# Two more turns in the hand-written matmul order, key norms read by strips, and a new order of small matmuls in each steady turn of a windowed-attention layer

## The chip, the cores and the metric

The kernel runs on one core of one Trainium2 chip, in fp32. The metric is the device time of one execution in microseconds (us), as the median of several runs. A core has TensorE (PE, matrix products), VectorE (DVE), ScalarE (ACT), GpSimd (POOL) and SyncE (SP, which here issues the DMAs). [...] the other data lies in SBUF, and large or rearranged data in DRAM.

## The reference, cut to what matters

The network has four layers and is run on two images ("batches"). The change touches only the first layer, an attention in which every pixel looks at the 3x3 pixels around it ("taps") and at pooled tokens of the whole image. Cut to what matters:

```python
q = (xf @ W_q + b_q).reshape(B, N, nh, hd).transpose(0, 2, 1, 3)
q_norm = _l2norm(q)
q_scaled = (q_norm + query_embedding[None]) * jax.nn.softplus(temperature)[None]
kv = xf @ W_kv + b_kv
...
k_l = _l2norm(k_l.reshape(B, N, nh, hd)).reshape(B, N, C)
...
attn_local = jnp.einsum('bhnd,bhndk->bhnk', q_scaled, k_local)   # k_local: 3x3 shifts of k
...
attn_pool = jnp.einsum('bhnd,bhpd->bhnp', q_scaled, _l2norm(k_pool))
attn = jax.nn.softmax(jnp.concatenate([attn_local, attn_pool], axis=-1), axis=-1)
a_local, a_pool = (attn[..., :ll], attn[..., ll:])
lt = jnp.einsum('bhnd,hdk->bhnk', q_norm, learnable_tokens) + learnable_bias[None] + a_local
x_local = jnp.einsum('bhnk,bhndk->bhnd', lt, v_local)             # v_local: 3x3 shifts of v
x_pool = jnp.einsum('bhnp,bhpd->bhnd', a_pool, v_pool)
xo = (x_local + x_pool).transpose(0, 2, 1, 3).reshape(B, N, C)
out = (xo @ W_proj + b_proj).reshape(B, C, H, W)
```

There are 512 channels, 8 heads of 64 channels, and 64x64 = 4096 pixels.

## The kernel before, in words

**Tiling.** A 128-channel group holds two heads. The pixels of one group are cut into four pieces of 1024 (`UT`), each of two blocks of 512 (`TB`). A piece of a group is a *unit*; there are 16, and each runs through a pipeline of stages. The loop in `run` (L2045 to L2090) makes turns i = -4 to 16. In turn i several stages work on different units: the projections make queries and keys of unit i+3 (and values of unit i+1), the tap products and tap sums belong to unit i+1, the attention to unit i, and the weighing of the taps to unit i-1.

**Stages**, with the lines that the text speaks of:
- `projections` (matmuls of `project`, L134: four per block of 512; ScalarE takes them out of PSUM, with squares for the norms, L2370 to L2376, values L2472). In a steady turn the order is first key block ("k0"), second key block ("k1"), the two query blocks, with values between.
- `norms` (L2410 to L2435): one matmul group sums the squares, which marks the start of a turn in what follows. VectorE makes inverse roots (L2413 to L2425). The inverses of the keys go by DMA to a small DRAM array, `inverse` (L2434); those of the queries are spread by a matmul and multiplied in by `normed` (L2445, L2448), and `learned` then multiplies the queries with the learned tokens (L2462, taken out at L2465) and scales them (L2467).
- `tap_products` and `tap_sums`: ScalarE copies the scaled queries to PSUM (L2483), VectorE multiplies them with shifted keys (L2489; in steady turns two taps in one instruction, the ninth alone, into two product buffers in turn). TensorE sums each product over the channels of a head (L2527) into the one "tap" bank, in pairs of taps. The bank is then multiplied by the inverse key norms, read back from DRAM (`tap_inverses`, L2513, L2536), and ScalarE takes its exponential (L2538).
- `attend`: scores with the pooled tokens (L2555), exponentials (L2559), values (L2565, copied out at L2567). GpSimd adds halves of the exponentials (L2574). The denominators are summed by matmuls (L2581 from the halves, L2584 from the taps). VectorE turns them (L2609), inverts (L2611), turns them back (L2612), multiplies the taps' weights (L2616) and adds the learned products (L2617). The weights are then spread by DMA to the rows of a heads' buffer (L2622).
- `weigh`: for each of ten rows of weights (the pooled part and nine taps), the row is fetched by DMA, spread over 64 partitions (`fetch_tap`, L2640). ScalarE copies its two halves into two PSUM banks (L2656), VectorE multiplies each with the shifted values (L2664; L2661 for the first row), and GpSimd adds the result to the unit's output (L2669). The finished unit is stored (L2675).
- `output` (L2252 to L2258): the layer's last product, from turn 14 on.

**What sets the order.** `in_turn` (L51) asks the stages of a turn in round robin for their next step, so each `yield` in a stage shifts what it issues after it by a step. In turns with `self.steady` set, TensorE's instructions keep exactly that order (`manual_schedule` on PE). The order on every other engine, and on TensorE in the other turns, is made by a scheduler from its own estimates. Tiles come from pools: five PSUM banks are shared by projections, scores, values, denominators, learned products and the copies of `weigh`; a matmul that takes a bank waits until its former user has been read. Each engine takes its instructions in order. SP issues its DMAs in order too.

**The inverse norms in DRAM.** `inverse` has, for each group of 128 channels, six rows of 4096 pixels with a margin: for two heads the three shifts by one column, all written by one DMA per block (row i is the same data, one element further). To scale the tap sums, twelve DMAs per unit read six rows each (four tile positions times three shifts by one image row).

Of the kernel before, what the change touches and what calls it, by code (L numbers as in the profile page):

```python
# [18 lines left out]
KC = C // P  # L19
# [1948 lines left out]
class Local:  # L1968
# [9 lines left out]
    def __init__(self, net, X, Y, sp_scale, d, wp, yp, pp, ppt, pps):  # L1978
        self.net, self.nc, self.vec, self.cst = net, net.nc, net.vec, net.cst
        self.X, self.Y, self.sp_scale, self.d = X, Y, sp_scale, d  # L1980
        self.wp, self.pp, self.ppt, self.pps = wp, pp, ppt, pps
        nc, new = self.nc, lambda shape, name: wp.tile(shape, F32, name=name)

        self.yd = yp.tile([P, KC, N], F32, name="yd")
        self.edge = W + 1
        self.inverse = yp.tile([6 * KC, N + 2 * self.edge], F32, name="inverse")
        self.wd = yp.tile([3, P, KC, C], F32, name="wd")
        self.rows = cycle([yp.tile([P // 2, self.UT], F32, name=f"rows{i}") for i in range(2)]).__next__

        R = W + 2  # L1990
        flat = Y.rearrange("p k n -> p (k n)")
        self.next_w = flat[:, :KC * C].rearrange("p (kc o) -> p kc o", kc=KC)
        whole = Lent(flat)
        self.kx, self.vx = (whole.take([P, R, R]) for _ in range(2))
        qs, self.kraw = whole.take([P, 3 * self.UT]), whole.take([P, self.UT])
        self.qs = [qs[:, i * self.UT:(i + 1) * self.UT] for i in range(3)]
        weighed = whole.take([P, 2 * self.UT])

        self.taps = ([weighed[:, i * self.UT:(i + 1) * self.UT] for i in range(2)]
                     + [new([P, self.UT], "tap2")])  # L2000
        self.prods = [new([P, 2, self.UT], f"prods{i}") for i in range(2)]
        self.tok = whole.take([P, KC, 32])
        late = new([P, 13 * TB + 3 * TB], "late")
        part = Lent(late)
        self.prob = part.ring([P, TB], 4)
        self.att = part.ring([P, self.UT], 2)
        self.els = part.ring([P, TB], 2)

        self.halves = [part.take([P, TB]) for _ in range(2)]
        self.recip = part.take([P, TB])  # L2010
        self.lts = part.ring([P, TB], 3)

        self.first = Lent(late[:, :12 * TB])
        self.gelus = Lent(late[:, 13 * TB:]).ring([P, TB], 3)
        self.raw_w = [w.rearrange("p (kc o) -> p kc o", kc=KC)
                      for w in (weighed, flat[:, 6144:8192])]
        self.w_sr = qs[:, :KC * C].rearrange("p (kc o) -> p kc o", kc=KC)
        self.fold = flat[:, :6144].rearrange("p (i kc o) -> p i kc o", i=3, kc=KC)
        self.kp = new([P, KC, NK], "kp")
        self.vp = new([P, 2, C], "vp")  # L2020
        self.qn = whole.take([P, self.UT])
        self.w3 = new([P, 3, KC, P], "w3")
        self.sq = [new([P, TB], f"sq{i}") for i in range(4)]
        self.half = new([P, 32], "mhalf32")
        self.qb = new([P, KC], "qe_scaled")
        self.bias = {i: new([P, KC], "b_" + i) for i in "qkv"}
        self.w, self.lt, self.el, self.out = {}, {}, {}, {}
        load = lambda w, src: nc.sync.dma_start(w, src.rearrange("(kc p) o -> p kc o", p=P))
        load(self.w_sr, d["W_sr"])
        for i, src in enumerate((d["W_q"], d["W_kv"][:, :C], d["W_kv"][:, C:])):  # L2030
            load(self.fold[:, i], src)
        for i in range(2):
            load(self.raw_w[i], d["W_kv"][:, i * C:(i + 1) * C])
        nc.sync.dma_start(self.tok, d["tok32"])
        nc.vector.memset(self.half, -0.5)

        nc.vector.tensor_tensor(self.qb, self.vec[:, V_QE:V_QE + KC], sp_scale, ALU.mult)
# [9 lines left out]
    def run(self):  # L2047


        self.nmean = self.net.stats[:, 0]  # L2050
        xs = self.pooled_tokens()
        heads = self.pooled_heads(xs)
        units = KC * self.UN
        unit = lambda u: u if 0 <= u < units else None
        self.pending = []
        for i in "qkv":
            self.fetch(i, 0)
        for i in range(-4, units + 1):
            made, ahead, u, before = (unit(i + n) for n in (3, 1, 0, -1))
            self.steady = 1 <= i < units - 4  # L2060
            streams, ended = [], []
            stages = [self.norms(streams, ended)]
            if ahead is not None:
                stages.append(self.tap_products(ahead))
            if u is not None:
                stages.append(self.attend(u))
            if i == units:
                stages.append(self.output(KC - 2))
            if before is not None:
                stages.append(self.weigh(before))  # L2070
            if ahead is not None:
                stages.append(self.tap_sums(ahead))
            values = ([ahead] if i > 0 and ahead is not None else
                      {-4: [0], -2: [1]}.get(i, []))
            stages.append(self.projections(made, values, streams))
            stages.append(self.normed(ended))
            if i < -2:
                stages.append(islice(heads, 12 if i == -4 else None))
            if i == units - 3:
                stages.append(self.fetch_output())  # L2080
            if units - 3 < i < units:
                stages.append(self.output(i - units + 2))
            if self.steady or i == units:
                with self.net.tc.manual_schedule(engines={mybir.EngineType.PE}):
                    in_turn(*stages)
            else:
                in_turn(*stages)

        self.nc.sync.dma_start(self.next_w, self.d["w_q1"].rearrange("(kc p) o -> p kc o", p=P))
        in_turn(self.output(KC - 1))  # L2090
# [3 lines left out]
    def pooled_tokens(self):  # L2094
# [35 lines left out]
                nc.sync.dma_start(self.wd[i], w3)  # L2130
        self.frame(self.kx)
        nc.gpsimd.memset(self.kraw[:, :TB], 0.0)
        for at in (0, self.edge - 1 + N):
            nc.sync.dma_start(self.inverse[:, at:at + self.edge + 1],
                              self.cst[:6 * KC, :self.edge + 1])
        return xs

    def pooled_heads(self, xs):
# [220 lines left out]
    def projections(self, u, uvs, streams):  # L2359
# [25 lines left out]

            uvs = [last - 1, last]
        values = [(u, j) for u in uvs for j in range(2)]
        made, taken = ((4, 6, 7, 8), (0, 2)) if self.steady else ((6, 7, 8, 9), (0, 3, 6, 9))
        for step in range(10):
            if step in made:  # L2390
                i = made.index(step)
# [8 lines left out]
    def norms(self, streams, ended):  # L2400
# [25 lines left out]
        for s, (which, u, j, part, _) in enumerate(before):  # L2426
            row = rows[32 * s:32 * s + 2, :]
            if which == "q":
                ended.append((s, row, u, j, part))
                continue  # L2430
            at = self.edge + 1 + u % self.UN * self.UT + j * TB
            a = self.inverse[u // self.UN * 6:][:2, at:at + TB]
            heads, cols = a.ap
            nc.sync.dma_start(bass.AP(a.tensor, a.offset, [heads, [2 * heads[0] - 1, 3], cols]),  # L2434
                              bcast(row, 1, 3))  # L2435
        yield

    def normed(self, ended):

        nc = self.nc  # L2440
        for _ in range(3 if self.steady else 5):
            yield
        mine = [(e, self.bank()) for e in ended]
        for (s, rows, *_), ps in mine:
            nc.tensor.matmul(ps, self.cst[32 * s:32 * s + 2, C_ROW:C_ROW + P], rows, start=True,  # L2445
                             stop=True)
        for (*_, part), ps in mine:
            self.multiplied = nc.vector.tensor_tensor(part, part, ps, ALU.mult).ins  # L2448
        for _ in range(3 if self.steady else 2):
            yield  # L2450
        if mine:
            self.learned(mine[-1][0][2])
        yield
# [52 lines left out]
    def tap_inverses(self, u):  # L2506
# [1 line left out]
        inverse = (self.kraw[:, :TB] if u < KC * self.UN - 1  # L2508
                   else self.w3[:, 2].rearrange("p k o -> p (k o)"))
        for q in range(4):  # L2510
            for dy in range(3):
                at = u % self.UN * self.UT + q // 2 * TB + dy * W + 1
                self.nc.sync.dma_start(inverse[32 * q + 6 * dy:][:6, :],  # L2513
                                       self.inverse[u // self.UN * 6:][:6, at:at + TB])
        return inverse

    def tap_sums(self, u):
# [24 lines left out]
    def attend(self, u):  # L2542
# [58 lines left out]
            halved(1)  # L2601
        yield
        values(1)
        yield
        if not self.steady:
            yield
        psD = sums()

# [7 lines left out]
        nc.vector.tensor_tensor(el, el, self.recip, ALU.mult)  # L2616
        nc.vector.tensor_tensor(el, el, self.lt.pop(u), ALU.add)  # L2617
        if self.steady:
            yield
        self.spread = self.rows()  # L2620
        for j in range(2):
# [244 lines left out]
```

## Time and profile before

| | us |
|---|---|
| median of 3 runs | 5019.44 (5018.5 to 5019.69) |
| the profiled execution | 5015.88 |
| its span in the trace | 5014.0 |
| a steady turn of layer 0 (turn 6, batch 0) | 41.48 |
| turn 11, turn 12 (start to next start) | 43.76, 51.05 |
| turn 13's start to the first output matmul (L2258) | 50.66 |
| TensorE busy in the span | 4771.4 |

In the trace layer 0 of the first batch has its steady turns (1 to 11) from 305.5 us to 764.1 us of the span, and the first output matmul at 865.8 us; the second batch's layer 0 lies later in the span and has the same turns. The page gives busy time by engine, 40 slices, DMA queues, a chain of waits, and groups of instructions. The other views are answers of the trace: busy time of every engine in given stretches, the instructions of one engine in order of time, and the waits of a stretch. In a timeline line stand the start, the duration, the engine, the line of the code, the operation and its tiles, the number of instructions joined in the line ("x2"), and in brackets the idle time before it and what ended that. In a line of waits stand the waiting engine and line, what released it, the sum in us, the number and the longest.

### The profile page before, as it was taken

The numbers are of one execution on the slowest core, as the hardware profiler recorded it, in microseconds if no ns is written. First come the engines' busy times: TensorE is split into PE (matmuls) and PEld (weight loads), VectorE is DVE, ScalarE is ACT, GpSimd is POOL, SyncE is SP. The second block draws the span as 40 slices with busy tenths as digits, with TensorE's granted clock in tenths as the row PEclk, the third lists the DMA queues.
The fourth block names the chain that finished last, engine by engine and source line by source line (L and its number), as shares of the span: only waits on it lengthen the run. The fifth ranks groups of instructions, "written<-read, shape, count | busy, mean of one in ns | idle before, by whom it ended". The sixth has DMA issues, their size and how long they took to land. (4 is left out here: it accounts for less than half of the span.)

```text
span 5014.0 us, 48290 instructions
## 1 busy us (share of the span) xinstructions
PE 4771.4 (95%) x16883; PEld 1971.8 (39%) x16883; DVE 3074.1 (61%) x3958; ACT 1816.8 (36%) x3477; POOL 1859.1 (37%) x1220
## 2 busy tenths in 40 slices
PE   7999998999999999999999999989999999999998
PEld 3433332554334444433343333335543344444333
DVE  4367776744679533477732777767446794335776
ACT  1256664244323233322112566642443242333221
POOL 0046665501320145554500466654014101554554
PEclk9999999999999999999999999999999999999999
DMA  3035555500000000211120455555000000000111
GB/s 154 1 103 155 155 156 164 160 19 10 1 17 0 1 1 1 72 55 44 58 74 2 126 154 157 151 159 150 12 10 1 17 1 1 1 1 24 43 45 43
DMA packets 129440, 313.29 MB, mean 62 GB/s; under 512 B 23394, under 2 KB 36194, under 8 KB 127652
## 3 DMA queue, kind: packets, MB, share of 16 engines
q1 hardware_dynamic: 129188, 310.12, 21.6%
q8 instruction: 135, 2.21, 0.2%
q14 instruction: 117, 0.96, 0.1%
HBM read 260.73 MB, written 49.31 MB: 62 GB/s over the span
## 5 line engine op out<-in xcount | busy, mean ns | idle before, releaser
L134 PE MATMUL mm<-big,w 128*128 128x512 f32 x2496 | 1164.9, 610 | 16.3 <-DVE big L2448 11.5
L134 PEld LDWEIGHTS mm<-big,w 128*128 128x128 f32 x2496 | 452.6, 191 | 698.3 <-issue 557.2
L2669 POOL TENSOR_TENSOR late<-late,big 128x1024 f32<-128x1024 f32 x194 | 458.5, 2363 | 223.4 <-DVE big L2664 185.4
L2489 DVE TENSOR_TENSOR prods<-qs,big 128x1024 f32<-128x1024 f32 (+1 forms) x200 | 332.2, 1686 | 60.1 <-PE tap L2527 49.1
L1669 POOL TENSOR_TENSOR big<-big 128x512 f32<-128x512 f32 x224 | 277.8, 1273 | 219.4 <-ACT big L1660 219.4
L2664 DVE TENSOR_TENSOR big<-big,mm 128x512 f32<-128x512 f32 x388 | 253.1, 681 | 114.9 <-ACT mm L2656 107.0
L1660 ACT ACTIVATE big<-mm,ed 128x256 f32<-128x256 f32 x512 | 193.5, 489 | 233.1 <-DVE top L1656 200.7
L2656 ACT COPY mm<-big 128x512 f32<-128x512 f32 x432 | 245.8, 597 | 60.4 <-DMA big<-rows 25.1
L2574 POOL TENSOR_TENSOR late<-late 128x512 f32<-128x512 f32 x84 | 105.3, 1275 | 410.5 <-ACT late L2559 393.9
L2669 POOL TENSOR_TENSOR late<-late,tap 128x1024 f32<-128x1024 f32 x94 | 222.1, 2363 | 94.5 <-DVE tap L2664 80.1
L1472 POOL TENSOR_TENSOR wq<-prob 128x512 f32<-128x512 f32 x48 | 71.6, 1515 | 487.9 <-ACT prob L1469 476.5
L1656 DVE TENSOR_REDUCE top<-mm 128x1 f32<-128x512 f32 x256 | 159.0, 684 | 148.1 <-PE mm L1587 148.1
L1924 PE MATMUL mm<-k,w 128*128 128x512 f32 x512 | 235.1, 602 | 12.4 <-DVE k L1917 7.5
L134 PE MATMUL mm<-big,wq 128*128 128x512 f32 x512 | 236.7, 608 | 2.7 <-ACT off_t L1243 2.7
L1215 PE MATMUL mm<-big,wo 128*128 128x512 f32 x512 | 238.1, 611 | 0.0
L1382 PE MATMUL acc<-big,diag 128*128 128x512 f32 x512 | 228.7, 604 | 9.8 <-ACT diag L1387 4.6
L1634 PE MATMUL mm<-w,big 128*128 128x512 f32 x512 | 234.5, 601 | 0.0
L973 POOL TENSOR_TENSOR group_stats<-group_stats,cst 128x1 f32<-128x1 f32 (+1 forms) x20 | 20.2, 1025 | 566.4 <-DVE group_stats L972 510.2
L2527 PE MATMUL tap<-prods,cst 128*32 128x512 f32 x1152 | 189.6, 620 | 29.2 <-ACT late L2538 26.5
L1914 DVE RECIPROCAL psD<-psD 128x512 f32<-128x512 f32 x64 | 215.1, 3362 | 1.9
L134 PE MATMUL mm<-big,big 128*128 128x512 f32 x464 | 201.7, 594 | 0.5 <-DVE b_sr L1011 0.5
L1469 ACT ACTIVATE prob<-mm 128x512 f32<-128x512 f32 x256 | 133.2, 603 | 171.4 <-PE mm L1466 171.1
(428 smaller groups left out, 8114.1 us busy)
## 6 DMA issues: line engine op xcount, KB each, us to landing
big<-rows SPq DMA_DIRECT2D x432, 256.0 KB
tap<-rows SPq DMA_DIRECT2D x208, 256.0 KB
yd<-late SPq DMA_DIRECT2D x32, 512.0 KB
lost_all<-lost SPq DMA_DIRECT2D x128, 128.0 KB
out<-big SPq DMA_DIRECT2D x64, 256.0 KB
big<-in_W_kv SPq DMA_DIRECT2D x8, 1024.0 KB
rows<-late SPq DMA_DIRECT2D x64, 128.0 KB
big<-in_x SPq DMA_DIRECT2D x32, 256.0 KB
```

Source lines behind the costliest of these rows:

```text
L134: self.nc.tensor.matmul(ps, w[:, kc, :], X[:, kc, blk * TB:(blk + 1) * TB], start=(kc == 0), stop=(kc == KC - 1))
L1215: nc.tensor.matmul(ps, w[:, kc, oc * P:(oc + 1) * P], att[:, kc, :], start=(kc == 0), stop=(kc == KC - 1))
L1382: nc.tensor.matmul(accs[b], dg, src[:, b * TB:(b + 1) * TB], start=(j == 0), stop=(j == 6))
L1634: nc.tensor.matmul(ps, X[:, kc, lo:lo + P], wv[:, kc, :], start=(kc == 0), stop=(kc == KC - 1))
L1660: nc.scalar.activation(f[:, t, :], pS[h][i][:, t % 2, :], AF.Exp, bias=ed[:, t, 2 * cc + h:2 * cc + h + 1])
L1669: nc.gpsimd.tensor_tensor(a, a, part, ALU.add)
L1914: nc.vector.reciprocal(psD, psD)
L1924: nc.tensor.matmul(ps, self.wo[:, kc, oc * P:(oc + 1) * P], qs[:, kc, :], start=(kc == 0), stop=(kc == KC - 1))
L2489: self.nc.vector.tensor_tensor(self.pair(u, k)[:, :n].rearrange("p k (y x) -> p k y x", x=W), bcast(qs.rearrange("p (y x) -> p y x", x=W), ...
L2656: nc.scalar.copy(ps, part)
L2664: nc.vector.tensor_tensor(part.rearrange("p (y x) -> p y x", x=W), self.vx[:, y:y + self.UY // 2, dx:dx + W], ps.rearrange("p (y x) -> p y ...
L2669: nc.gpsimd.tensor_tensor(out, out, t, ALU.add)
```

## The change

Four edits, all in the class `Local`:
- *More steady turns.* `steady` holds for turns 1 to 13 instead of 1 to 11. The tuple that places the projections of values gets two more places (`taken`), which only turn 13 uses, as it projects the values of two units.
- *Norms by strips.* `inverse` has 18 rows per group instead of six: the three shifts by an image row are stored too. Each block is written by three DMAs instead of one, and each unit reads four times 18 rows instead of twelve times six. The margin cleared at the beginning is wider.
- *Order of small matmuls in steady turns.* `attend` goes on to the denominators directly after the second values, without a step between; so they come ahead of the third tap pair (taps 4 and 5). `normed` makes the learned products a step earlier, right behind that tap pair. Before, the order was: second values, third tap pair, denominators, k1, learned products, first query block. Now it is: second values, denominators, third tap pair, learned products, k1, first query block.
- *A later spread.* In steady turns `attend` makes one more step before it issues the spread of the weights (L2622).

```diff
-        self.inverse = yp.tile([6 * KC, N + 2 * self.edge], F32, name="inverse")
+        self.inverse = yp.tile([18 * KC, N + 2 * self.edge], F32, name="inverse")
...
-            self.steady = 1 <= i < units - 4
+            self.steady = 1 <= i < units - 2
...
-        for at in (0, self.edge - 1 + N):
-            nc.sync.dma_start(self.inverse[:, at:at + self.edge + 1],
-                              self.cst[:6 * KC, :self.edge + 1])
+        for at in (0, N):
+            nc.sync.dma_start(self.inverse[:, at:at + 2 * self.edge],
+                              self.cst[:18 * KC, :2 * self.edge])
...
-        made, taken = ((4, 6, 7, 8), (0, 2)) if self.steady else ((6, 7, 8, 9), (0, 3, 6, 9))
+        made, taken = ((4, 6, 7, 8), (0, 2, 4, 6)) if self.steady else ((6, 7, 8, 9), (0, 3, 6, 9))
...
-            at = self.edge + 1 + u % self.UN * self.UT + j * TB
-            a = self.inverse[u // self.UN * 6:][:2, at:at + TB]
+            at = 2 * self.edge + u % self.UN * self.UT + j * TB
+            a = self.inverse[u // self.UN * 18:][:2, at:at + TB]
             heads, cols = a.ap
-            nc.sync.dma_start(bass.AP(a.tensor, a.offset, [heads, [2 * heads[0] - 1, 3], cols]),
-                              bcast(row, 1, 3))
+            row_at = heads[0]
+            for dy in range(3):
+                nc.sync.dma_start(bass.AP(a.tensor, a.offset + dy * (6 * row_at - W),
+                                          [heads, [2 * row_at - 1, 3], cols]), bcast(row, 1, 3))
...
-        for _ in range(3 if self.steady else 2):
+        for _ in range(2):
             yield
         if mine:
             self.learned(mine[-1][0][2])
...
         for q in range(4):
-            for dy in range(3):
-                at = u % self.UN * self.UT + q // 2 * TB + dy * W + 1
-                self.nc.sync.dma_start(inverse[32 * q + 6 * dy:][:6, :],
-                                       self.inverse[u // self.UN * 6:][:6, at:at + TB])
+            at = self.edge + u % self.UN * self.UT + q // 2 * TB
+            self.nc.sync.dma_start(inverse[32 * q:][:18, :],
+                                   self.inverse[u // self.UN * 18:][:18, at:at + TB])
...
         values(1)
-        yield
         if not self.steady:
+            yield
             yield
         psD = sums()
...
         if self.steady:
+            yield
             yield
         self.spread = self.rows()
```

## The prediction, made before the changed kernel was run

> **What bounds the kernel now.** First the page's head: which engine is full. Then busy time by stretches of one batch of layer 0, with each turn's start as boundary. All times are of one profiled execution. A turn's own clock, T, is us after the start of its norms matmul (L2410); the typical steady turn (turn 6) starts at 471.40.
>
> ```profile
> PE 4771.4 (95%) x16883; PEld 1971.8 (39%) x16883; DVE 3074.1 (61%) x3958; ACT 1816.8 (36%) x3477; POOL 1859.1 (37%) x1220
> ```
> ```profile
> core 0: us, PE busy (x) PEld busy (x) DVE busy (x) ACT busy (x) POOL busy (x), PEclk, DMA share, GB/s
> 471.40:512.88 41.48, 40.78 (x149) 12.86 (x148) 32.52 (x48) 25.59 (x45) 26.25 (x13) 1.00 0.60 160
> 720.31:764.07 43.76, 42.69 (x159) 13.24 (x159) 34.86 (x52) 25.45 (x45) 26.25 (x13) 1.00 0.58 156
> 764.07:815.12 51.05, 46.38 (x155) 14.65 (x155) 32.83 (x53) 25.74 (x45) 26.13 (x13) 0.93 0.52 145
> 815.12:865.78 50.66, 41.69 (x157) 11.53 (x157) 36.02 (x57) 24.21 (x44) 30.38 (x17) 0.90 0.64 172
> ```
> A steady turn is TensorE from end to end: 40.78 of 41.48 us busy, 0.70 idle. The stretches that begin with turns 11, 12 and 13 (the last ends at the first output matmul, L2258) take 43.76, 51.05 and 50.66, together 145.47. There TensorE waits. The waits of the last two name two long ones, and the timelines say why:
>
> ```profile
> PE tap L2527 <- ACT late L2538: 12.5, 2, 8.2
> ```
> ```profile
> 788.34 4.72 SPq L2513 DMA_DIRECT2D big<-inverse  x12
> ```
> ```profile
> 844.36 2.37 DVE L2616 TENSOR_TENSOR late<-late 128x512 f32<-128x512 f32 x1
> 846.77 0.69 DVE L2617 TENSOR_TENSOR late<-late 128x512 f32<-128x512 f32 x1
> 847.38 0.69 DVE L2536 TENSOR_TENSOR tap<-tap,big 128x512 f32<-128x512 f32 x1
> ```
> The tap bank is scaled by L2536 and read by the exponential L2538 before the next unit's tap sums may enter it. In turn 12 twelve row reads take SP from 788.3 to 793.1; in turn 13 L2536 stands on VectorE behind L2609 to L2617. These cost 4.23 and 8.23 us.
>
> Now the block that the change rearranges, in the steady turn, on TensorE and VectorE:
>
> ```profile
> 490.45 1.06 PE L2527 MATMUL tap<-prods,cst 128*32 128x512 f32 x8
> ...
> 493.32 1.08 PE L2584 MATMUL mm<-late,cst 64*64 64x512 f32 x4
> 494.32 3.70 PE L134 MATMUL mm<-big,w 128*128 128x512 f32 x8
> 497.96 1.06 PE L2462 MATMUL mm<-big 128*32 128x512 f32 x8
> ```
> ```profile
> 491.61 1.22 DVE L2489 TENSOR_TENSOR prods<-qs,big 128x1024 f32<-128x1024 f32 x1
> 492.74 1.27 DVE L2664 TENSOR_TENSOR big<-big,mm 128x512 f32<-128x512 f32 x2
> 494.44 0.73 DVE L2609 STREAM_TRANSPOSE mm<-mm 128x512 f32<-128x512 f32 x1 [0.43 <-PE mm L2584]
> ...
> 496.36 2.06 DVE L2616 TENSOR_TENSOR late<-late 128x512 f32<-128x512 f32 x1
> 498.45 0.69 DVE L2617 TENSOR_TENSOR late<-late 128x512 f32<-128x512 f32 x1
> ```
> ```profile
> 493.09 4.78 POOL L2669 TENSOR_TENSOR late<-late,big 128x1024 f32<-128x1024 f32 x2
> ```
> The last tap product (491.61) and three taps' weighing multiplies (L2664, pairs from 489.22, 490.41, 492.74) are done before the denominators' transpose L2609 (494.44, T 23.04). Nothing that TensorE wants next is queued behind that chain: the second key projection ("k1", L134 at 494.32) starts without a gap.
>
> [...] a first L134 matmul after another tile form takes 0.53 us from start to start against 0.43 inside a run, and about 0.1 shows at the end of a small-tile block. [...] L2616 took 0.69 us in turns where no POOL add ran, 2.06 here, ending 0.55 after POOL's add. [...] a dependent second norm write left 3.0 us after the first (480.2, 483.2).
>
> **The change, part by part.** I read the order of instructions in both built programs, turn by turn; that order has no times, which I put in from the rows above.
>
> *Fewer form changes, steady turns.* TensorE's work is the same, but denominators follow the second values (both 64-row tiles) and the learned products follow the third tap pair (both 128*32). From the blocks' steps in the trace I count 0.47 us less per turn: sums start at T 18.96, tap pair 21.76, learned 22.66, and k1 could start at 23.66. From k1's start to the turn's end TensorE has 17.36 us: 41.02 if nothing stalls.
>
> *The new wait.* k1's bank is the one that a weighing copy (L2656) used, and is free only after the first half of that tap's multiply ("B"). Before, that bank's last reader was L2567, done at T 19.8. In the new order VectorE runs L2609 as soon as the sums end: L2609 21.87 to 22.6, L2611 to 23.0. Then comes the last tap product, which needs the product buffer of the third tap pair, now behind the sums: 22.92 to 24.14. L2612 ends at 24.77. Then two patterns, as the scheduler placed it: in turns 1, 2, 5, 6, 9, 10, 13, L2616 (POOL idle, 0.69) to 25.49 and B after that, to 26.15; in turns 3, 4, 7, 8, 11, 12, B at once, to 25.4. ScalarE doesn't help: in the first pattern its copy for B stands behind the query copy L2483, which waits for that last product. So k1 starts 2.5 or 1.8 us late, and all of TensorE's turn behind it (the rest of k1, both query projections, tap sums, scores, values, the next turn's norms) with it. First pattern: 26.15 + 17.36 = 43.5, +2.03 on 41.48. Second: 25.43 + 17.36 = 42.8, +1.3; there L2617 may lie behind a POOL add, as L2616 does here, and then the first query projection waits up to 1.2 more for the next tap's multiply: 44.0, +2.5. What hid all this before was that the multiplies ran ahead of L2609. Turns 1 to 10 per batch: 6 x 2.03 + 4 x (1.3 to 2.5) = 17.4 to 22.2 us lost.
>
> *Strips.* Norm writes to DRAM go from 2 to 6 a turn, reads back from 12 to 4: SP has fewer issues (14 to 10). But the writes stand in a row, the last three behind the landing of the first: about 8.8 to 12.6 on T with the 3.0 us above, so the fetch of the next tap's rows, issued at 10.1 now, moves to about 12.7. Its copy reads it at 16.7 at the earliest: covered; without the cover it would be 0 to 2.6 us a turn. Landing of 18 rows in one read isn't in the trace: [...] it has over 8 us before L2536. In steady turns I take 0. The spread of the weights (L2622) is issued one step later; its data, L2617's result, is ready at about 27.4 against 27.7 now: 0. The larger initial clear adds two small DMAs' bytes, before the loop: 0 to 1 us, I take 0.
>
> *Turns 12 and 13 steady.* Turn 13 also projects four values, one at every other step, which is the work it had. The stretches of 11 and 12 become second-pattern turns of 42.8 to 44.0. From turn 13's start to L2258 VectorE sets the pace: from L2609 at T 21.9 it has some 26 us of work to its last tap inverse (single products of 1.22, the multiplies of 0.68, the chain), and the output's matmul follows at about 50.5. Sum 136 to 138.5 against 145.47: 7 to 9.4 saved per batch. The twelve-read wait (4.23) goes; of the 8.23, VectorE's own work keeps most.
>
> *Sum.* Per batch 17.4 to 22.2 lost and 7 to 9.4 saved: 8 to 15 slower; two batches, +16 to +31, I take +26. The profiled execution is 5015.88 (span 5014.0 and 1.9 around it), so 5042; the median shown, 5019.44, is 3.6 above it, so 5045. Likeliest case's own range 5032 to 5055.
>
> **The rivals.**
> - *It does what it says (faster).* One mechanism: B's multiply finds its place before L2609, so that k1 doesn't wait. The deciding point is k1's start: at T 24.5 a steady turn is 0.4 longer and the end pays for it; at 23.7 each gains 0.47. Then 10 x 0.47 + 9 to 18 (up to the removal of both tap waits) per batch, 27 to 45 in all: 4974 to 4992, say 4985. For: TensorE is at 95% and VectorE has 9 us idle a turn. Against: the trace follows the built order on every engine, and B stands behind the transposes in every steady turn.
> - *Balance (within 0.2%).* The wait is there but shorter, about 1.2 a turn, since the last product leaves early or the copy isn't late; the end saves 12. Per batch 10 x 0.8 to 10 x 1.5 against -12: between -4 and +3, twice; 5011 to 5025. Against: B's earliest end is a sum of measured durations.
> - *A second limit on top.* POOL's adds move with the multiplies (its fifth starts at about 26.8 instead of 21.7, leaving 3 us to the turn's end), or the write burst makes a tap late: 1 us more a turn, 20 in all: 5065 to 5080. [...] against: those 3 us.
> - *The form changes alone.* Strips and the new end do nothing that shows: then 4.7 us gained per batch, inside rival one.
>
> **How the numbers follow.** About 0.2%, 10 us, is what a measurement here can tell from no change. Slower as summed, 0.60; second limit, 0.12; balance, 0.15; faster, 0.13. So faster 0.13, same 0.15, slower 0.72. The range takes in the likeliest case, most of the balance and the foot of the second limit: 5010 to 5068.
>
> **What would show it.** In the profile after: a wait of L134 on VectorE's L2664 in nearly every steady turn, 1.8 to 2.5 us long, and turns of 42.8 to 44.0; L2616 at 0.69 us in six of ten; the wait of tap sums on L2538 gone in turn 12 and shorter in 13; the end 136 to 138.5. If steady turns are 41.0 long, rival one holds; above 44.5, the second limit. I am wrong if B runs before the transposes, or the end saves over 15 us per batch.

## The result, and the profile after

The changed kernel takes 5078.61 us (median of 4 runs, 5073.34 to 5083.70) against 5018.97 for the kernel before (median of 4, 5012.85 to 5019.69): 59.6 us more, a ratio of 1.012 with a 95% interval of 1.0108 to 1.0132. The forecast was 5045 with a range of 5010 to 5068. The direction was right; the loss was forecast at 26 us and is more than twice that.

The profiled execution after took 5077.93 us, with a span of 5076.1, 62.1 more than before. Cut at the same marks as in the prediction, the difference comes from here (us, batch 0 and batch 1):

| stretch of layer 0 | before | after | forecast | measured |
|---|---|---|---|---|
| turns 1 to 10 | 414.9, 414.8 | 444.3, 445.9 | +17.4 to +22.2 | +29.5, +31.0 |
| turn 11 to first output matmul | 145.5, 144.3 | 140.2, 139.8 | -7 to -9.4 | -5.2, -4.6 |
| first to last output matmul | 149.1, 149.1 | 152.9, 151.8 | 0 | +3.7, +2.6 |

These sum to +57.1. The remaining 5 lie outside, 3.3 of them between the first batch's last output matmul and the second batch's first turn, a stretch that takes 1683.6 to 1697.3 us in these runs although their kernels are alike there.

The page's head of the kernel after. TensorE's busy time grew by only 6.0 us. That is a net figure: a steady turn at full clock has 0.40 us less work (40.38 busy in turn 6 after, 40.78 before), while a lowered clock, shown below, makes the same work take longer (turn 1 has 42.07 us busy with the clock at 0.96). Most of the loss is waiting:

```profile
PE 4777.4 (94%) x16883; PEld 1980.5 (39%) x16883; DVE 3065.8 (60%) x3942; ACT 1819.6 (36%) x3477; POOL 1869.2 (37%) x1220
```

Busy time by stretches after: turns 1, 6, 11, 12 and turn 13 up to the first output matmul (the column after POOL's is TensorE's granted clock).

```profile
core 0: us, PE busy (x) PEld busy (x) DVE busy (x) ACT busy (x) POOL busy (x), PEclk, DMA share, GB/s
305.52:350.75 45.23, 42.07 (x150) 13.73 (x149) 31.09 (x48) 25.46 (x45) 26.58 (x13) 0.96 0.49 131
528.80:572.34 43.54, 40.38 (x150) 13.14 (x149) 31.20 (x50) 25.47 (x45) 26.58 (x13) 1.00 0.58 149
749.84:793.78 43.94, 40.61 (x150) 13.06 (x149) 33.24 (x49) 25.73 (x46) 26.55 (x13) 1.00 0.56 143
793.78:837.74 43.96, 40.62 (x150) 13.06 (x149) 32.71 (x48) 24.64 (x44) 26.59 (x13) 1.00 0.60 163
837.74:890.08 52.34, 42.91 (x174) 11.29 (x173) 38.82 (x59) 25.28 (x45) 30.92 (x17) 0.97 0.67 195
```

Turn 6 shows the forecast wait. Its start is at 528.80 (the turn at 471.40 that the prediction calls turn 6 is the fifth by this count; in the kernel before turns 1 to 10 are alike to 0.01 us, so nothing hangs on it). Here are TensorE, VectorE and ScalarE around the rearranged block (lines of the kernel after are one or two higher than before: L2610 to L2618 are the denominators' chain, L2666 the multiply, L2491 the tap product, L2485 the query copy, L2658 the weighing copy, L2464 the learned products):

```profile
550.58 1.06 PE L2528 MATMUL tap<-prods,cst 128*32 128x512 f32 x8
551.47 1.04 PE L2464 MATMUL mm<-big 128*32 128x512 f32 x8
554.98 5.42 PE L134 MATMUL mm<-big,w 128*128 128x512 f32 x12 [2.47 <-DVE big L2666]
```
```profile
550.70 0.73 DVE L2610 STREAM_TRANSPOSE mm<-mm 128x512 f32<-128x512 f32 x1 [2.80 <-PE mm L2585]
551.47 0.37 DVE L2612 RECIPROCAL mm<-mm 128x32 f32<-128x32 f32 x1
551.74 1.21 DVE L2491 TENSOR_TENSOR prods<-qs,big 128x1024 f32<-128x1024 f32 x1
552.87 0.70 DVE L2613 STREAM_TRANSPOSE late<-mm 128x512 f32<-128x512 f32 x1
553.60 0.69 DVE L2617 TENSOR_TENSOR late<-late 128x512 f32<-128x512 f32 x1
554.23 1.29 DVE L2666 TENSOR_TENSOR big<-big,mm 128x512 f32<-128x512 f32 x2
```
```profile
553.04 0.59 ACT L2485 COPY qs<-big 128x512 f32<-128x512 f32 x1 [4.45 <-DVE prods L2491]
553.56 1.10 ACT L2658 COPY mm<-big 128x512 f32<-128x512 f32 x2
```

k1 starts at T 26.17 after 2.47 us of idle time (forecast: 26.15 and 2.5). The chain stands in the forecast order, down to the last tap product between L2612 and L2613. VectorE idles for 2.80 us just before it: the multiply had room there, but its copy on ScalarE stood behind L2485, which waited for that product.

Turn 1 has the same wait and is 1.7 us longer still. By stretches of one us, k1 running (it starts at 331.69):

```profile
331.00:332.00 1.00, 0.31 (x1) 0.30 (x2) 1.00 (x3) 1.00 (x3) 0.00 (x0) 1.00 0.02 8
332.00:333.00 1.00, 1.00 (x3) 0.40 (x2) 0.83 (x2) 1.00 (x3) 0.63 (x1) 0.75 0.00 0
333.00:334.00 1.00, 1.00 (x3) 0.47 (x2) 0.91 (x2) 0.51 (x1) 1.00 (x1) 0.50 0.00 0
...
335.00:336.00 1.00, 1.00 (x2) 0.34 (x1) 0.00 (x0) 0.00 (x0) 0.92 (x2) 0.54 0.00 0
336.00:337.00 1.00, 1.00 (x4) 0.46 (x3) 0.00 (x0) 0.00 (x0) 1.00 (x1) 1.00 0.58 213
```

TensorE is busy throughout and shows no wait once k1 runs, yet the clock falls to half for 3.41 us, from 332.50 to 335.91 (so the slices at both ends show 0.75 and 0.54). None of this is idle time, so no list of waits names it.

With this, turns 1 to 10 of batch 0 add up: six first-pattern turns at +2.05 and four second-pattern turns at +2.45 give 22.1; three turns with a lowered clock (1, 2, 9) add 1.70 each, 5.1; weight rows of a tap that reach ScalarE late add 2.3 in turns 5 and 9. Sum 29.5. Batch 1: 22.1, four lowered turns (1, 2, 6, 10) 6.8, and 2.1 left, 1.1 of it in turn 5 and put to late rows too: 31.0.

### The profile page after: what moved, and what is told of

It is laid out like the page before. It is cut to its first block, busy times and chain, and to the rows that moved or that the text cites. A ratio compares the mean times of both kernels' runs of the same rounds, so it can differ in the third digit from the quotient of the medians.

```text
span 5076.1 us, 48115 instructions
## 1 busy us (share of the span) xinstructions
PE 4777.4 (94%) x16883; PEld 1980.5 (39%) x16883; DVE 3065.8 (60%) x3942; ACT 1819.6 (36%) x3477; POOL 1869.2 (37%) x1220
## 3 DMA queue, kind: packets, MB, share of 16 engines
q8 instruction: 135, 2.21, 0.2%
## 5 line engine op out<-in xcount | busy, mean ns | idle before, releaser
L2491 DVE TENSOR_TENSOR prods<-qs,big 128x2048 f32<-128x2048 f32 (+1 forms) x184 | 330.5, 1817 | 25.8 <-PE tap L2528 15.3
L2666 DVE TENSOR_TENSOR big<-big,mm 128x512 f32<-128x512 f32 x388 | 253.9, 681 | 151.3 <-ACT mm L2658 109.9
L2658 ACT COPY mm<-big 128x512 f32<-128x512 f32 x432 | 244.0, 591 | 152.1 <-DMA big<-rows 110.0
```

The source lines that it names most:

```text
L2491: self.nc.vector.tensor_tensor(self.pair(u, k)[:, :n].rearrange("p k (y x) -> p k y x", x=W), bcast(qs.rearrange("p (y x) -> p y x", x=W), ...
L2658: nc.scalar.copy(ps, part)
L2666: nc.vector.tensor_tensor(part.rearrange("p (y x) -> p y x", x=W), self.vx[:, y:y + self.UY // 2, dx:dx + W], ps.rearrange("p (y x) -> p y ...
```

## The experiments

The theories at the outset. A: the new order and the strips do the harm together, by the place of the fifth tap's multiply on VectorE. B: the order alone does it. C: the strips' six writes do it by themselves. D: what the end gains is always given back in the output. For the rest of the loss, G: TensorE's idle stretch itself lowers the clock afterwards; H: the clock falls for another reason. Ratios are against the kernel before, run beside each.

### 1. The order alone

```diff
 # on the kernel before
-        for _ in range(3 if self.steady else 2):   # normed
+        for _ in range(2):
...
         values(1)
-        yield
         if not self.steady:
+            yield
             yield
...
         if self.steady:
+            yield
             yield
         self.spread = self.rows()
```


> The kernel before with the new order of small matmuls alone (denominators right behind the second values, learned products a step earlier, the later spread); norms not by strips, turns 12 and 13 not steady. Theory A (the order and the strips do the harm together: only with both does the built program put the fifth tap's multiply behind the denominators' transpose on VectorE): here that multiply stands before the transpose, so k1 finds its bank free; steady turns of 41.0 to 41.1 us, 11 of them by 0.4 to 0.47 shorter in two batches: about 5009 us. Theory B (the order alone does it): turns of 43.5 and 43.9 us with a k1 wait of 1.7 to 2.5 us, about 5075 us.

Measured: 5011.96 us against 5016.07, ratio 0.9993 (0.9986 to 1.0). B falls: there is no loss. In turn 6 (from 512.01) the fifth tap's multiply stands ahead of the denominators' transpose on VectorE, and k1 starts at 535.64 (T 23.63) without a wait:

```profile
532.31 0.69 DVE L2665 TENSOR_TENSOR big<-big,mm 128x512 f32<-128x512 f32 x1 [0.41 <-ACT mm L2657]
533.90 0.73 DVE L2609 STREAM_TRANSPOSE mm<-mm 128x512 f32<-128x512 f32 x1 [0.90 <-PE mm L2584]
```

The whole of this turn, all engines:

```profile
512.01:553.00 40.99, 40.29 (x149) 13.14 (x148) 31.75 (x49) 25.93 (x46) 26.60 (x13) 1.00 0.60 161
```

41.0 us, as A said. The total gained less than A's 10 us because turns 5 and 9 came to 41.8 to 42.9 (in turn 9 of batch 0 ScalarE waits 6.0 us for rows of taps), and turn 11 of batch 1 to 46.4, against 43.8 before. The total alone can't be told from no gain; turns 1 to 10 took 1.2 and 2.2 us less than before.

### 2. The strips alone

Edit: the `inverse` lines of the change, with the old order and turns 1 to 11 steady.

> The kernel before with the norms by strips alone (18 rows a group, six writes and four reads a turn). Theory A: steady turns stay at 41.5 us, since the later tap fetch has cover in the old order; turn 12's wait of 4.2 us for twelve reads shrinks by 0 to 4 us: 5011 to 5019 us. Theory C (the row of six writes on SP is the harm by itself, as it delays the taps' rows): steady turns longer by 1 us or more with ScalarE's copies waiting for DMA, over 5035 us.

Measured: 5034.65 against 5016.07, ratio 1.0036 (1.0022 to 1.0049). Both expectations miss. The loss is C's in size, but not for C's reason. Turn 6 (from 519.75), TensorE and then ScalarE:

```profile
543.77 2.41 PE L134 MATMUL mm<-big,w 128*128 128x512 f32 x5 [1.03 <-DVE big L2665]
```
```profile
541.22 1.21 ACT L2485 COPY qs<-big 128x512 f32<-128x512 f32 x2 [1.68 <-DVE prods L2491]
542.36 1.10 ACT L2657 COPY mm<-big 128x512 f32<-128x512 f32 x2
```

The fifth tap's copy (L2657) stands behind the query copies on ScalarE and runs straight after them, without a wait for DMA; its multiply follows at 543.03 and k1 at 543.77, 1.03 us late. The steady turns are 42.58, 1.1 more (three of the 20 from 1 to 10 take another 0.3 to 0.5). In the kernel before, that copy ran ahead of the query copies. So the strips move the copy to a later place in ScalarE's order.

### 3. The steady turns alone

```diff
 # on the kernel before
-            self.steady = 1 <= i < units - 4
+            self.steady = 1 <= i < units - 2
...
-        made, taken = ((4, 6, 7, 8), (0, 2)) if self.steady else ((6, 7, 8, 9), (0, 3, 6, 9))
+        made, taken = ((4, 6, 7, 8), (0, 2, 4, 6)) if self.steady else ((6, 7, 8, 9), (0, 3, 6, 9))
```


> The kernel before with turns 12 and 13 steady, alone (and the two places for values). Theory A: the stretches of turns 11 and 12 become 41.5 us each (2.3 and 9.5 less), turn 13 stays near 50.5 us, the output may take up to 3 us more: 9 to 13 us less per batch, 4993 to 5001 us. Theory D (the end's gain is always given back in the output's turns): within 5 us of 5019.

Measured: 4993.88 against 5016.07, ratio 0.9958 (0.9945 to 0.9972). As A expected: turns 11 and 12 at 41.48. Turn 13 is 53.7 and 53.4, 3 longer, but the output is 2 shorter (147.4, 146.8). From turn 11 to the last output matmul 284.0 and 283.2 us, against 294.6 and 293.5 before. D falls here.

### 4. The changed kernel with the fifth tap's multiply first

```diff
 # on the kernel after
-            held = (self.net.tc.issue_after(self.multiplied) if self.steady and k == 4
-                    else nullcontext())
+            held = (self.net.tc.issue_after(self.multiplied if k == 4 else self.turned)
+                    if self.steady and k in (4, 8) else nullcontext())
...
         psD = sums()
-        nc.vector.transpose(psD, psD)
+        held = nullcontext()
+        if self.steady:
+            yield
+            held = self.net.tc.issue_after(self.weighed)   # the multiply of tap 5
+        with held:
+            self.turned = nc.vector.transpose(psD, psD).ins
```

One of the two steps ahead of the spread is taken out for it, so the spread keeps its place.

> The changed kernel, all edits kept and TensorE's order the same; on VectorE alone the fifth tap's multiply is put before the denominators' transpose and the last tap product behind it. Theory A: k1 starts near 23.7 us of the turn, steady turns 41.0 to 41.3 us, no lowered clock in steady turns: 5079 less about 60 for turns 1 to 10 and about 10 for turns 11 and 12: 5005 to 5012 us if turn 13 and the output stay as they are. Theory C (SP's write burst makes the tap's rows land late, the place on VectorE is only a sign of that): the multiply waits for its rows, k1 still starts at 25 us or later, over 5050 us.

Measured: 4996.90 against 5016.07, ratio 0.9963 (0.9949 to 0.9977). With all edits of the change in place, the order of TensorE untouched, and SP writing its six strips, the loss turns into a gain. Turn 6 (from 512.93), VectorE and TensorE:

```profile
533.30 1.28 DVE L2669 TENSOR_TENSOR big<-big,mm 128x512 f32<-128x512 f32 x2 [1.27 <-issue]
534.83 0.73 DVE L2614 STREAM_TRANSPOSE mm<-mm 128x512 f32<-128x512 f32 x1 [0.25 <-PE mm L2585]
```
```profile
535.59 1.04 PE L2464 MATMUL mm<-big 128*32 128x512 f32 x8
536.57 4.99 PE L134 MATMUL mm<-big,w 128*128 128x512 f32 x11
```

The multiply runs at T 20.4, ahead of the chain; k1 starts at 23.64 without a gap, and the turn is 41.00 us (forecast for a stall-free one: 41.02). The rows of the tap were there in time, so C falls as the cause of the change's loss. Turns 5 and 9 are again 42.2 to 43.7, one of them with a lowered clock. The total is 8 us under the expected range; turn 13 is uneven, 49.3 and 55.9 us. The multiply's copy on ScalarE moved ahead of the query copies with it (532.61 and 537.29), so the run shows the place of copy and multiply together, and not which of the two queues decides.

### 5. The change without the strips

Edit: experiments 1 and 3 together.

> The changed kernel without the strips: norms written and read as before, the new order and steady turns 12 and 13 kept. Theory A (order and strips harm together): steady turns of 41.0 us through turn 12, except turns 5 and 9, which may be 1.4 to 1.9 longer as in the run with the order alone; turn 13 near 53.5 as in the run with the steady turns alone: 4985 to 4991 us, under both single edits. Theory B (the order costs where the end is steady too): above 5000 us.

Measured: 5001.60 against 5018.01, ratio 0.9962 (0.9948 to 0.9976). The total misses A's range and lies where B was put (above 5000), so it doesn't decide between them. The turns do: they are 41.0 as A expected, and there is no loss. But the gain isn't the sum of the two, and the kernel is no faster than experiment 3. Turns 5 and 9 are 42.6 and 45.5 in batch 0, 44.7 and 44.7 in batch 1, three of the four with a lowered clock: what the order gains in the other turns is lost in these. Turn 13 of batch 1 also took 56.8 us, against 53.4 in experiment 3.

### 6. The same with the earlier spread

```diff
 # on experiment 5
         if self.steady:
-            yield
             yield
         self.spread = self.rows()
```


> As the run without strips, and the weights' spread issued a step earlier again, as before the change. Theory E (the later spread makes the rows of the next unit's taps late in turns 5 and 9, where the weights of a new channel group are loaded too): turns 5 and 9 fall to 41.0 to 41.3 us, 3 us less per batch than without strips, 4979 to 4985 us. Theory F (the weight loads alone make them late): turns 5 and 9 stay 1.4 to 1.9 longer, same time as without strips.

Measured: 5266.94 against 5018.01, ratio 1.0497 (1.0483 to 1.0512). Both theories E and F fall by far. Turn 6 (from 569.02), SP, then ScalarE:

```profile
599.57 1.18 SPq L2622 DMA_DIRECT2D rows<-late  x2
603.69 2.38 SPq L2640 DMA_DIRECT2D big<-rows  x4
```
```profile
608.48 1.11 ACT L2656 COPY mm<-big 128x512 f32<-128x512 f32 x2 [10.82 <-DMA big<-rows]
```

The spread (L2622) now stands ahead of the current unit's row fetches on SP. Next to be issued is the fetch of the next unit's first row, which reads what the spread writes: it left 2.94 us after the spread was issued (600.75 to 603.69); the rows that ScalarE needs come behind. TensorE waits 9.2 us a turn. So, with norms not by strips, the new order costs 5% unless the spread is issued later too.

### 7. The change without the order

Edit: experiments 2 and 3 together.

> The changed kernel with the old order of small matmuls and the old spread: strips, and steady turns 12 and 13. If what the strips cost alone adds to what the steady turns gain alone: turns 1 to 12 of 42.6 us with a k1 wait of 1.0 us, no lowered clock in them, 4994 plus 1.1 times 24, about 5015 to 5021 us. If the strips pay at the end (four reads for twelve): turn 13 under 52 us and 5005 to 5012.

Measured: 5028.60 against 5018.01, ratio 1.0025 (1.0017 to 1.0032). Turns of 42.59 with a k1 wait of 1.03 us and no lowered clock, as expected (turns 5 and 9 up to 43.8). The total is 8 us over the expected 5015 to 5021. Turn 13 is 51.5 and 51.8, about 2 us shorter than in experiment 3, but the output takes 154.5 against 147: the strips cost at the end too.

### 8. Work added in the idle time

```diff
 # on the kernel after, in learned
-                nc.tensor.matmul(ps[32 * q:32 * q + 32, :], self.tok[:, cc, :],
-                                 qn[:, j * TB:(j + 1) * TB], start=True, stop=True)
+                for _ in range(2 if self.steady else 1):
+                    nc.tensor.matmul(ps[32 * q:32 * q + 32, :], self.tok[:, cc, :],
+                                     qn[:, j * TB:(j + 1) * TB], start=True, stop=True)
```


> The changed kernel, with each learned-product matmul of steady turns issued twice (the second overwrites the first with the same values), 0.9 us of added TensorE work inside the idle time ahead of k1. Theory G (the lowered clock in seven of the first-pattern turns is set off by an idle stretch of about 1.9 us or more in one 3.41 us window): the idle falls from 2.47 to about 1.6, no lowered clock in turns 1 to 12, first-pattern turns all at 43.5, second-pattern ones at 43.9: 5065 to 5070 us although work was added. Theory H (the clock falls for another reason): some turns still at 45.2 us, 5077 us or more.

Measured: 5073.69 against 5018.01, ratio 1.011 (1.0095 to 1.0126). The total can't be told from the change's own 1.012, as turn 13 grew to 59.0 and 58.1. The turns decide. Turn 1, with PE's line in it:

```profile
305.94:349.47 43.53, 41.26 (x157) 13.48 (x157) 30.79 (x48) 25.58 (x45) 26.57 (x13) 1.00 0.46 125
```
```profile
332.11 2.41 PE L134 MATMUL mm<-big,w 128*128 128x512 f32 x5 [1.57 <-DVE tap L2667]
```

k1 starts at the same 26.17; only the idle time is 1.57 instead of 2.47. Turns 1 and 2 both fall from 45.2 to 43.53, and no turn from 1 to 12 has a lowered clock. G holds; H falls.

### 9. The old order where weights are loaded

```diff
 # on experiment 5: early = self.steady and i % 4 != 0 takes the place of steady
 # in the three edits of the order
+            self.early = self.steady and i % 4 != 0
```


> The run without strips, but in turns 4, 8 and 12 (in which the next channel group's weights are loaded on SP) the old order and the old place of the spread. If the later spread behind those loads is what makes turns 5 and 9 long: turns 4, 8, 12 at 41.5 us, 5 and 9 at 41.0 to 41.5, all others 41.0: 1.0 to 4 us less per batch than with the steady turns alone, 4985 to 4992 us, the fastest kernel here. If the loads alone make them long: turns 5 and 9 still 42.5 us or more, 4995 to 5000 us.

Measured: 4989.42 against 5019.96, ratio 0.9944 (0.993 to 0.9957), the fastest median here, though its interval overlaps those of experiments 3 and 4. Turns 5 and 9 are 41.0 to 41.2 (one other turn of each batch is 1.1 to 1.5 long). So what made them long was the new order with its later spread in the turns that load the next group's weights (4 and 8). The loads alone don't do it (41.48 in the kernel before), nor do order and spread without loads (41.0). Whether it is the order or the spread isn't separated here, since both went back to the old form in these turns.

### 10. The change with the learned products behind k1

```diff
 # on the kernel after
-        for _ in range(2):   # normed
+        for _ in range(3 if self.steady else 2):
```


> The changed kernel, with the learned products put back behind k1 (denominators still right behind the second values). k1 then takes the bank of the denominators' or an earlier tile and waits for VectorE's chain through L2613 (end at about 24.8 us of the turn) in place of the fifth tap's multiply; the learned products wait for that multiply, which is done before k1 ends. Theory A (the denominators ahead of the third tap pair are what puts a wait on k1, the learned products only decide which one): k1 starts at 24.8 to 25 us, turns of 42.2 to 42.7 us, idle under 2.2 us: 5079 less 1 to 1.5 us in each of 24 turns and less most of the low-clock stretches: 5025 to 5050 us. Rival (the learned products ahead of k1 are the harm): no wait of k1 over 0.5 us, turns of 41 us, about 5005 us.

Measured: 5067.44 against 5019.96, ratio 1.0099 (1.0083 to 1.0114). k1 starts at T 24.91, as A expected, now behind L2613:

```profile
PE mm L134 <- DVE late L2613: 2.1, 1, 2.1
```

The rival falls. The expected turn was too short, and so was the expected total of 5025 to 5050: the learned products now come after the wait, so their 1.1 us are in the turn too: 24.91 + 17.36 + 1.1 = 43.4, and 43.44 was measured. Of 24 turns eight have a lowered clock.

## Why the prediction was right in direction and wrong in size

- **The new wait: right.** Forecast starts of k1 were 26.15 and 25.43; measured 26.17 and 25.39. Forecast turns 43.5 and 42.8 to 44.0; measured 43.53 and 43.94. The second pattern came out near its upper end because L2617 (now L2618) did lie behind a POOL add: it began 0.49 us after the add and took 2.73, ending 0.54 after it, against 0.68 in the first pattern, where it began 0.22 ahead of the add; this made the first query projection wait 0.95. Without lowered clocks and late rows the loss is 22.1 per batch, the top of the forecast 17.4 to 22.2.
- **The failed step, the price of the stall: "From k1's start to the turn's end TensorE has 17.36 us".** That held at full clock only. The stall was priced at its length, not at what it does to the work after it. In seven of the twelve first-pattern turns from 1 to 10 the clock fell to half for 3.41 us: 1.70 each, 11.9 us in all. The clock column stood in the prediction's own table (0.93 and 0.90 in turns 12 and 13, the ones with long waits) and was not used.
- **How much each term was off.** Against the middle of the forecast (19.8 lost and 8.2 saved per batch) layer 0 lost 33.9 us more over both batches: 13.0 at the end (turn 11 and after), 11.9 by the lowered clock in turns 1 to 10, 4.6 by the stall itself, 4.4 by late rows. Some 5 us lie outside layer 0. So the end was mis-sized as much as the stall.
- **The second failed step, the end: the sign right, the size wrong.** Turns 11 and 12 are 43.9, in the forecast range. Turn 13 came to 52.3 and 51.9 against 50.5, with a k1 wait of 2.47 and lowered clocks in it, and the output was taken as unchanged but grew by 3.7 and 2.6. From turn 11 to the last output matmul the change saves 1.5 and 1.9 us, not 7 to 9.4. The runs point to the strips with turn 13 steady for the output's growth: it takes 150.6 to 154.5 in the kernel after and in experiments 4, 7, 8 and 10, which have both, and 146.4 to 149.9 without that pair, save in experiment 6 with its late rows (154.2 and 150.5). By which wait was not tried.
- **Strips: "In steady turns I take 0": wrong.** Alone they cost 1.1 us a turn (experiment 2). This did not put the sum off, as the stall was read from the order built with both edits. But the prediction read the place of the multiply as the new order's doing. It is the pair's: with the order alone the multiply stays ahead of the transpose (experiment 1), with both it goes behind. That the scheduler's estimate of SP's later fetch is what moves it is argued, not shown; shown is that the real rows were in time (experiment 4).
- **The later spread: 0 was right for most turns.** In turns 5 and 9, after the weight loads, the change lost 0.3 to 1.5 us beyond the stall and the lowered clock. In experiment 5 these turns were 1.6 to 4.5 too long; experiment 9 puts this to the new order and the later spread with the loads, not to the spread alone.
- **The rivals.** "It does what it says" names the right point: with k1 at 23.64 (experiment 4) the kernel is faster, at 4997 against the 4974 to 4992 worked out. "A second limit on top" (5065 to 5080) holds the measured time, but by luck: with the six writes kept, turns of 41.0 us were reached (experiment 4), so neither POOL nor the writes bounded them.

## What to carry to other kernels

When an edit moves one engine's work, read the built order of the other engines as well: here TensorE's new order was worth 0.48 us a turn (41.48 to 41.00), and the place of one tap's copy and multiply on ScalarE and VectorE decided between that and a loss of 2. Edits made at once need their combination tried: alone, the order gave -4 us (no sure change), the strips +19 and the steady turns -22, which sum to -8; all together gave +60. The position of the multiply behind the transpose came only with order and strips together. Price a stall on a full TensorE at its length plus what the clock takes afterwards (here 1.70 us after 7 of 12 waits of about 2.5 us, none after 12 waits of 1.57), and read the clock column next to the waits.

## What the runs showed of the hardware

In the kernel after, the clock record of the profiled execution has 39 stretches at 0.50: 26 of 3.41 us, 12 of two to four times that, and one that runs past the end of the span. All start on one fixed grid of 3.41 us through the whole execution. In turns 1 to 12 of that kernel there are 24 k1 waits over 1.5 us: the seven with at least 2.21 us in one window of the grid were followed by half clock, the 17 with at most 1.86 us were not. With the same turns of experiments 8 and 10 there are 60 such waits: every one with at least 2.02 us in one window was followed by half clock (15), and none with at most 1.86 us was (45). So a wait of 2.47 us was followed by half clock or not by where it fell: the one before 331.69 lay in one window whole (half clock), the one before 554.98 had 1.86 us in one and 0.61 in the next (clock 1.00). As an estimate, with the limit taken at 1.95, between the two measured figures: a wait of 2.47 has that much in one window for (3.41 - 2.47) + 2 x (2.47 - 1.95) = 1.98 of every 3.41 us, 58% of positions; 7 of 12 were hit, one of them at a wait of 2.82. The waits of 1.57 us in experiment 8 lie under that limit wherever they fall, and none of the 12 was followed by half clock.

These figures hold for these waits only. In other parts of the kernel less idle time was followed by half clock too: in the kernel before TensorE is busy for 2.27 of the 3.41 us from 1455.10 to 1458.51, 1.14 idle, and the window after it has a clock of 0.50. What else lowers the clock there was not tried.
